# Self-attention denominators added up on Pool, and the context's split in the added tile's memory

## The chip, the cores and the metric

The kernel runs on one core of a Trainium2 chip. The metric is the device time of one execution in microseconds. A core has five engines with instruction queues of their own: TensorE (PE in the profile; PEld are its weight loads), VectorE (DVE), ScalarE (ACT), GpSimd (POOL, called Pool here) and SyncE (SP), which issues most of the transfers. An engine executes its instructions in the order in which they were written to its queue, and an instruction waits for semaphores of other engines and of transfers.

## The reference

Six stages work on x of shape (4, 512, 512) and a context of shape (4, 512, 128). Each adds its result to x and applies a layer norm:

```python
x = _layernorm(x + _L0_attn_ref(x, ...))            # causal self-attention, 16 heads of 32
x = _layernorm(x + _L0_xattn_ref(x, ctx, ctx))      # cross-attention, 32 query heads, 8 key heads of 16
x = _layernorm(x + _L0_ffn_ref(x, ...))             # feed-forward with ternary weights
x = _layernorm(x + _L1_attn_ref(x, ...))            # causal self-attention, 16 heads of 32
x = _layernorm(x + _L1_xattn_ref(ctx, x, ...))      # adjacency: similarity, top 153 of 512 in each row
x = _layernorm(x + _L1_ffn_ref(x, ...))             # 16 experts, two per token, and one shared
```

The change is in the two self-attentions and in the cross-attention. A causal self-attention computes, for every head, `softmax(q k / sqrt(32))` over the keys that are not later than the query, times v. The softmax is the exponential of each score less the row's maximum, divided by the sum of these exponentials over the keys (the denominator).

The adjacency stage takes its similarities from the context alone, so its selection of the largest 30% in each row (a bisection on a threshold) can be made at any time; the kernel makes it beside the self-attentions.

## The kernel before

**Self-attention.** Queries are on the free axis and keys on the partitions when the exponentials are taken, so the denominator is a sum over partitions, and that is a matmul with ones. The work is cut into 16 groups n for each layer: batch b = n // 4, and four heads, g = n % 4. The 512 keys are four tiles kb of 128. Since the attention is causal, tile kb meets only the queries from 128 kb on: the score tiles of four heads are 512, 384, 256 and 128 queries wide. A loop runs over steps t, four for each group. In each step the following is issued:

- `maxima` (line 230 and on): the scores of one tile of queries, with the queries on the partitions, for a row maximum. DVE reads them with the mask (L246) into `st`.
- at the group's first step, `least`: the negative maxima are turned on TensorE and copied by ScalarE (`nmT`, L269).
- `softmax(n, kb)`: five steps after the maxima, with kb in the order 2, 1, 0, 3. TensorE computes the scores with keys on the partitions, adds the negative maximum and the mask by matmuls, and ScalarE writes the exponentials (L296) into the tile `p` of this kb, two heads at a time.
- at the group's second step, `values(n - 2)`: first the denominators (matmuls of `ones` and `p` into a `tp` tile of PSUM, copied by ScalarE to `us`, L311), then, after the step's softmax, the products with the values (`va`) into `mm`. `finish` takes the reciprocals (L324) and multiplies (L325).
- projections of the next batch (q through DVE, L216; k through ScalarE, L220; v through DVE, L222) and the output projection of the last one, a part in every step. In the first steps it is those of batch 0.
- `background()`: one step of the selection.

The scores use three pairs of PSUM banks, and `mm` and `tp` one bank each, so a matmul into any of these waits until the engine that reads its bank has done so. The order of all matmuls on TensorE is fixed as they are issued (`in_order`; the profile shows all of them at the helper's line L424). The other engines' orders are made by a scheduler at build time, by its own costs.

**The background.** In the first self-attention `background()` begins with `split_context` (L436 and on). For each batch it loads the context into `ct` on SP's queue (L442), and Pool scales it (L443), writes a bf16 part (L446), subtracts it (L449), and so on, for three parts. Each part is sent to DRAM, `ctx_part` (L447). `ct` and the three parts `ct0` to `ct2` are four tiles of their own. Then the parts are arranged in DRAM as the cross-attention's keys: `keys[0]` by eight transfers (L452), and `keys[1]` by 20: four times 16 rows of the third part (L458), and 16 transfers of ones (L462) into the other rows, from a tile that Pool sets (L456). Then the selections of batches 0 and 1 follow; in the second self-attention it is those of batches 2 and 3, without a split. A selection computes similarities on TensorE (`sim`), takes the rows' largest and smallest on DVE, the first midpoint on Pool (`mid`, L1015 and L1016), and then, step by step, counts signs on ScalarE (L1023) and moves the midpoint on Pool (L1031 to L1035).

Pool also adds the output bias to x in the self-attentions (L193).

**Cross-attention.** At its start DVE sets the tiles `va0` and `va1` to ones (L490) and three small tiles `xl` to zeros (L494), beside the last layer norm of the self-attention (L339 to L349). For each batch the keys come back from DRAM as `ks` (from `keys[0]`, L498) and `kl` (from `keys[1]`, all 128 partitions, L499). Pool splits the queries (L527 to L531), TensorE multiplies, and DVE takes the maxima (L554).

The lines of the helper behind each kind of sums, in `values`:

```python
for to, left in ((t, None), (o, VA[b % 2])):
    for kb in range(NT):
        for j in range(NJ):
            multiply(to[HD * j : HD * (j + 1), kb * P :], ...)
```

Of the kernel before, what the change touches and what calls it, by code (L numbers as in the profile page):

```python
# [21 lines left out]
P = 128  # L22
# [18 lines left out]
def decoder_kernel(ctx: ExitStack, tc: tile.TileContext, a: dict, out: bass.AP):  # L41
# [39 lines left out]
    iota_i = const.tile([P, NE], mybir.dt.int32, tag="iotai", name="iota_i")  # L81
    G.iota(iota_i, pattern=[[1, NE]], base=0, channel_multiplier=0)
    iota = const.tile([P, NE], F32, tag="iota", name="iota")
    V.tensor_copy(iota, iota_i)
    thr = const.tile([P, B * NT], F32, tag="thr", name="thr")
    ctx_parts = [tc.dram_tile([P, B * S], BF16, name=f"ctx_part{k}") for k in range(3)]
    keys = [tc.dram_tile([P, 8, B * S], BF16, name=f"keys{k}") for k in range(2)]
# [48 lines left out]
    def self_attention(pre, first, background=lambda: None):  # L136
# [3 lines left out]
        with tc.tile_pool(name=pre + "w", bufs=1) as wp, tc.tile_pool(  # L140
# [130 lines left out]
            PR = {}  # L271
# [25 lines left out]

            def values(n):

                b, g = divmod(n, NG)  # L300
                o, t = psum_mm(), psum_tp().rearrange("p n t -> p (n t)")
                for to, left in ((t, None), (o, VA[b % 2])):
                    for kb in range(NT):
                        for j in range(NJ):
                            multiply(
                                to[HD * j : HD * (j + 1), kb * P :],
                                ones[:, :HD] if left is None else left[:, kb, NJ * g + j, :],
                                PR[n, kb][:, j, :], start=(kb == 0), stop=(kb == NT - 1),
                            )
                    u = po.tile([P, S], F32, tag="us" if left is None else "u", name="u", bufs=1)  # L310
                    A.copy(u, to)  # L311
                    if left is None:
                        sums = u
                        yield
                if g == 0:
                    O[b] = po.tile([P, NG, S], F32, tag="oT", name="oT", bufs=1)
                F[n] = sums, u
# [119 lines left out]
    def split_context(pool):  # L437


        for b in range(B):  # L440
            ct = pool.tile([P, S], F32, tag="ct", name="ct")
            nc.sync.dma_start(ct, a["ctxT"][:, ts(b, S)])  # L442
            G.tensor_scalar(ct, ct, 0.25, None, ALU.mult)  # L443
            for k in range(3):
                c = pool.tile([P, S], BF16, tag=f"ct{k}", name=f"ct{k}")
                G.tensor_copy(c, ct)  # L446
                nc.sync.dma_start(ctx_parts[k][:, ts(b, S)], c)  # L447
                if k < 2:
                    G.tensor_tensor(ct, ct, c, ALU.subtract)  # L449
            yield  # L450
        for p, k in enumerate(KPART):
            nc.sync.dma_start(  # L452
                keys[0][ts(p, XD)], ctx_parts[k].rearrange("(g d) t -> d g t", d=XD)
            )
        one = pool.tile([P, S], BF16, tag="ct0", name="ct0")
        G.memset(one, 1.0)  # L456
        for r in range(P // 32):
            nc.sync.dma_start(  # L458
                keys[1][32 * r : 32 * r + XD], ctx_parts[2].rearrange("(g d) t -> d g t", d=XD)
            )  # L460
            for b in range(B):
                nc.sync.dma_start(  # L462
                    keys[1][32 * r + XD : 32 * (r + 1), :, ts(b, S)],
                    one[:XD].unsqueeze(1).to_broadcast([XD, XG, S]),
                )
        yield
# [7 lines left out]
    def cross_attention(background):  # L474
        HD, NG, NJ, NP = XD, XG, 4, XP
        multiply, transpose = in_order()
        with tc.tile_pool(name="ck", bufs=1) as kp, tc.tile_pool(
# [8 lines left out]
            for k in range(2):  # L486
                KS.append(kp.tile([P, NG, S], BF16, tag=f"ks{k}", name=f"ks{k}"))
                KL.append(kp.tile([P, NG, S], BF16, tag=f"kl{k}", name=f"kl{k}"))
# [8 lines left out]
            def load(b):  # L497
                nc.sync.dma_start(KS[b % 2], keys[0][:, :, ts(b, S)])  # L498
                nc.sync.dma_start(KL[b % 2], keys[1][:, :, ts(b, S)])  # L499
# [931 lines left out]
    with tc.tile_pool(name="sims", bufs=1) as mp:  # L1431
        selection, background = selecting((0, 1), mp, split_context(mp))
        with psum(3, 1, 1):
            self_attention("L0", True, background)
# [19 lines left out]
    with tc.tile_pool(name="sims2", bufs=1) as mp:  # L1454
        selection, background = selecting((2, 3), mp)
        with psum(3, 1, 1):
            self_attention("L1", False, background)
# [51 lines left out]
```

## Time and profile before

| what | value |
|---|---|
| median of 3 runs | 2528.08 us (2526.78 to 2528.53) |
| profiled execution | 2531.25 us, its span 2529.5 us |
| mean granted TensorE clock | 0.958 |
| first self-attention | 0 to about 546 us of the span |
| cross-attention | from about 546 us |
| second self-attention | about 1420 to 1960 us |
| Pool, busy over the span | 629.6 us (25%) |
| all transfers | 163.74 MB |

The profile is that of one execution. Its page gives each engine's busy time, then groups of instructions by line, engine and tile, with the number of instructions, the mean time of one in nanoseconds, and the idle time ahead of them with what ended it. A timeline row gives the start, the length, the engine, the line, the operation with its tiles and shapes, how many instructions it joins, and in brackets the idle time before it with its releaser. The view of waits adds up what an engine waited for: microseconds in total, how often, and the longest. TensorE shows a float32 matmul as two records, so the 16 matmuls of one block of sums are 32 records.

### The profile page before, as it was taken

The page shows a single profiled execution, that of the slowest core. Times are in us where ns is not written, and L with a number is a line of the kernel's source. Part 1 is how long each engine was busy: PE and PEld are TensorE (multiplying, and loading weights), DVE is VectorE, ACT ScalarE, POOL GpSimd, SP SyncE. Part 2 cuts the span into 40 slices and gives each one's busy share as a digit, 9 for nine tenths or more (in the row PEclk, how much of TensorE's full clock was granted, in tenths as well). Part 3 has the DMA queues.
Part 4 walks back from the last instruction along what each step waited for, and adds up shares of the span by engine and source line. Part 5 has one row for each costly group of instructions (what it writes and reads, how often), then busy time and mean ns, then how long its engine had stood idle before and what let it go on. Part 6 is the DMA issues. An engine that isn't in the chain of part 4 may idle for free. (4 is left out here: it accounts for less than half of the span.)

```text
span 2529.5 us, 34778 instructions
## 1 busy us (share of the span) xinstructions
PE 2263.4 (89%) x13014; PEld 1006.0 (40%) x13014; DVE 1424.4 (56%) x3136; ACT 1105.4 (44%) x1744; POOL 629.6 (25%) x1218
## 2 busy tenths in 40 slices
PE   7899999878989899989998689989998898999996
PEld 2334333333333333345555234433444443444442
DVE  2455565547887878758887345546555741111117
ACT  0732643325767677665665273274323210122221
POOL 7300210033333333137766240031000031000005
PEclk9999999889999999999999799999998899999997
DMA  6500000037130401000000200000001241444536
GB/s 221 152 22 18 1 17 1 1 125 242 48 119 22 146 1 51 1 1 1 1 1 1 85 5 14 1 1 20 1 1 51 68 167 66 134 133 152 181 119 197
DMA packets 93436, 163.74 MB, mean 65 GB/s; under 512 B 7376, under 2 KB 39504, under 8 KB 93264
## 3 DMA queue, kind: packets, MB, share of 16 engines
q1 hardware_dynamic: 76000, 122.94, 14.8%
q10 hardware_dynamic: 12144, 21.77, 2.3%
q0 software_dynamic: 5120, 16.78, 2.0%
q8 instruction: 103, 1.69, 0.3%
q14 instruction: 69, 0.57, 0.1%
HBM read 163.30 MB, written 51.64 MB: 85 GB/s over the span
## 5 line engine op out<-in xcount | busy, mean ns | idle before, releaser
L554 DVE TENSOR_REDUCE nm<-sc 128x2 f32<-128x1024 f32 x256 | 304.2, 1218 | 99.1 <-PE sc L424 98.8
L592 ACT ACTIVATE p<-sc 128x1024 f32<-128x1024 f32 x256 | 248.4, 1023 | 138.9 <-PE sc L424 138.9
L246 DVE CUSTOM_DVE_ANT_0 e<-sc,late_keys 128x256 bf16<-128x256 f32 (+3 forms) x512 | 222.5, 484 | 128.3 <-PE sc L424 128.3
L296 ACT ACTIVATE p<-sc 128x512 f32<-128x512 f32 (+3 forms) x256 | 165.8, 700 | 213.3 <-PE sc L424 213.3
L424 PE MATMUL mm<-p,va 128*32 128x512 f32 (+3 forms) x2048 | 217.6, 528 | 0.7 <-ACT p L592 0.5
L1363 PE MATMUL sc<-wug,xbT 128*128 128x512 f32 x376 | 185.2, 600 | 17.3 <-ACT sl L1368 14.1
L424 PE MATMUL sc<-qs,ks 128*128 128x512 bf16 x512 | 151.7, 382 | 33.7 <-DVE nm L554 31.8
L424 PE MATMUL sc<-ks,qs 128*128 128x512 bf16 x512 | 157.2, 391 | 4.4 <-DVE nm L554 3.3
L424 PE MATMUL sc<-kT,qT 32*128 32x512 f32 (+3 forms) x1024 | 133.7, 498 | 24.5 <-ACT p L296 20.4
L424 PE MATMUL sc<-qT,kT 32*128 32x256 f32 (+3 forms) x1024 | 133.9, 509 | 17.4 <-DVE st L246 15.6
L324 DVE RECIPROCAL u<-u 128x128 f32<-128x128 f32 x128 | 108.4, 909 | 62.0 <-ACT u L311 62.0
L1360 DVE COPY xbT<-tp 128x512 f32<-128x512 f32 x47 | 32.2, 689 | 196.2 <-PE tp L1358 196.2
L1023 ACT ACTIVATE junk<-sim,mid 128x512 bf16<-128x512 f32 x176 | 124.9, 722 | 17.2 <-POOL mid L1016 17.2
L1397 POOL DMA_INDIRECT yg<-ys,pi x32 | 35.2, 1099 | 375.8 <-issue 373.4
L746 POOL TENSOR_TENSOR y<-z 128x512 f32<-128x512 f32 (+1 forms) x48 | 97.3, 2040 | 87.3 <-DVE z L731 87.2
L424 PEld LDWEIGHTS sc<-kT,qT 32*128 32x128 f32 x1024 | 51.8, 189 | 116.5 <-issue 73.4
L424 PEld LDWEIGHTS <-ks 128*128 128x128 bf16 x512 | 50.0, 98 | 117.2 <-issue 76.7
L746 POOL TENSOR_TENSOR z<-y 128x512 f32<-128x512 f32 x64 | 95.3, 1508 | 3.4 <-issue 2.1
L1363 PEld LDWEIGHTS sc<-wug,xbT 128*128 128x128 f32 x376 | 64.9, 190 | 77.5 <-issue 54.6
L424 PEld LDWEIGHTS sc<-qT,kT 32*128 32x128 f32 x1024 | 52.0, 193 | 97.7 <-issue 58.6
L1377 PE MATMUL sc<-wd,hT 128*128 128x512 f32 x188 | 88.3, 592 | 0.0
L743 ACT ACTIVATE g<-sc,sg 128x512 f32<-128x512 f32 x64 | 43.7, 685 | 94.0 <-PE sc L734 62.3
(297 smaller groups left out, 4175.8 us busy)
## 6 DMA issues: line engine op xcount, KB each, us to landing
wug<-in_Wu SPq DMA_DIRECT2D x47, 512.0 KB
wug<-in_Wg SPq DMA_DIRECT2D x47, 512.0 KB
wd<-in_Wd SPq DMA_DIRECT2D x47, 512.0 KB
xs<-zero SPq DMA_DIRECT2D x3, 4096.0 KB
xb<-xs SPq DMA_DIRECT2D x47, 256.0 KB
ys<-yb ACTq DMA_DIRECT2D x47, 256.0 KB
w<-in_w_gate SPq DMA_DIRECT2D x16, 512.0 KB
w<-in_w_up SPq DMA_DIRECT2D x16, 512.0 KB
```

Of the source, the lines that this page charges most:

```text
L246: V.tensor_tensor_reduce(e, at[r], late_keys[:, (NT - m) * P :], 1.0, LOWEST, ALU.add, ALU.max, accum_out=st[:, i, r : r + 1],)
L296: A.activation(heads, sc[h][:, :, :m], AF.Exp)
L324: V.reciprocal(sums[:, ts(i, P)], sums[:, ts(i, P)])
L424: ins = op(*args, **kw)
L554: V.tensor_reduce(NM[n][:, i, 2 * h : 2 * h + 2], sc, AX.X, ALU.max, negate=True)
L592: A.activation(p[:, 2 * h : 2 * h + 2, :], sc[h], AF.Exp)
L743: then(act, A.activation(*args, **kw))
L746: then(pool, getattr(G, op)(*args))
L1023: A.activation(e, s[k], AF.Sign, bias=bias[:, k : k + 1], accum_out=to[:, k : k + 1])
L1363: T.matmul(pp[:, 0, :], xbT[:, c, :], wug[s][:, c, :, :].rearrange("p q f -> p (q f)"), start=(c == 0), stop=(c == NK - 1),)
L1377: T.matmul(pp[:, 1, :], hT[:, c, :], wd[s][:, c, :], start=(c == 0), stop=(c == F // P - 1),)
L1397: G.indirect_dma_start(out=y, out_offset=None, in_=ys, in_offset=bass.IndirectOffsetOnAxis(pos[k][:, t : t + 1], 0),)
```

## The change

The change has three parts.

First, the denominators. For queries of 128 and on, Pool now adds up the exponentials of the key tiles 0, 1 and 2 in a new tile `R` of 128 x 4 heads x 384 queries (tag `r`, one buffer, in the pool that also holds the similarities). After the exponentials of kb = 1 it adds those of kb = 2 to them (two adds of 2 heads x 256 queries); after those of kb = 0 it adds these (for each pair of heads one add of 2x128, one of 2x256). So six adds for each group. `values` then multiplies ones by p of kb = 0 for the first 128 queries, by R for the 384 others, and by p of kb = 3 for the last 128: 640 columns instead of 1280 for each head, 12 matmuls instead of 16. The products with the values stay as they were.

Second, `ct` and its three bf16 parts are slices of one tile that has R's tag and so R's one buffer. All the split's tiles and all R share this memory, one after another. The small integer tile `iota_i` also moves to a pool that is closed at once.

Third, `keys[1]` keeps only the 16 rows of the third part in DRAM, written by one transfer. DVE sets both `kl` tiles to ones at the start of the cross-attention, and for each batch four transfers of 16 rows replace the one of 128.

```diff
-    iota_i = const.tile([P, NE], mybir.dt.int32, tag="iotai", name="iota_i")
...
+    with tc.tile_pool(name="int", bufs=1) as ip:
+        iota_i = ip.tile([P, NE], mybir.dt.int32, tag="iotai", name="iota_i")
...
-    keys = [tc.dram_tile([P, 8, B * S], BF16, name=f"keys{k}") for k in range(2)]
+    keys = [tc.dram_tile([n, 8, B * S], BF16, name=f"keys{n}") for n in (P, 16)]
...
                     A.activation(heads, sc[h][:, :, :m], AF.Exp)
 
+                for h in range(NJ // 2):
+                    heads = slice(2 * h, 2 * h + 2)
+                    if kb == 1:
+                        if not h:
+                            R[n] = tiles.tile([P, NJ, S - P], F32, tag="r", name="r")
+                        G.tensor_tensor(
+                            R[n][:, heads, P:], p[:, heads, P:], PR[n, 2][:, heads, :], ALU.add
+                        )
+                    elif kb == 0:
+                        r = R[n][:, heads, :]
+                        G.tensor_tensor(
+                            r[:, :, :P], PR[n, 1][:, heads, :P], p[:, heads, P : 2 * P], ALU.add
+                        )
+                        G.tensor_tensor(r[:, :, P:], r[:, :, P:], p[:, heads, 2 * P :], ALU.add)
...
-                    for kb in range(NT):
+                    if left is None:
+                        parts = [(PR[n, 0][:, :, :P], 0), (R.pop(n), 1), (PR[n, 3], 3)]
+                    else:
+                        parts = [(PR[n, kb], kb) for kb in range(NT)]
+                    for p, q in parts:
                         for j in range(NJ):
                             multiply(
-                                to[HD * j : HD * (j + 1), kb * P :],
-                                ones[:, :HD] if left is None else left[:, kb, NJ * g + j, :],
-                                PR[n, kb][:, j, :], start=(kb == 0), stop=(kb == NT - 1),
+                                to[HD * j : HD * (j + 1), q * P : q * P + p.shape[2]],
+                                ones[:, :HD] if left is None else left[:, q, NJ * g + j, :],
+                                p[:, j, :],
+                                start=q < (2 if left is None else 1),
+                                stop=q == NT - 1 or (left is None and q == 0),
                             )
...
         for b in range(B):
-            ct = pool.tile([P, S], F32, tag="ct", name="ct")
+            all_ = pool.tile([P, 4, S - P], F32, tag="r", name="ct").rearrange("p j t -> p (j t)")
+            ct = all_[:, :S]
...
-                c = pool.tile([P, S], BF16, tag=f"ct{k}", name=f"ct{k}")
+                c = all_[:, S + k * (S // 2) : S + (k + 1) * (S // 2)].bitcast(BF16)
...
-        one = pool.tile([P, S], BF16, tag="ct0", name="ct0")
-        G.memset(one, 1.0)
-        for r in range(P // 32):
-            nc.sync.dma_start(
-                keys[1][32 * r : 32 * r + XD], ctx_parts[2].rearrange("(g d) t -> d g t", d=XD)
-            )
-            for b in range(B):
-                nc.sync.dma_start(
-                    keys[1][32 * r + XD : 32 * (r + 1), :, ts(b, S)],
-                    one[:XD].unsqueeze(1).to_broadcast([XD, XG, S]),
-                )
+        nc.sync.dma_start(keys[1], ctx_parts[2].rearrange("(g d) t -> d g t", d=XD))
...
-                KL.append(kp.tile([P, NG, S], BF16, tag=f"kl{k}", name=f"kl{k}"))
+                t = kp.tile([P, NG, S], BF16, tag=f"kl{k}", name=f"kl{k}")
+                V.memset(t, 1.0)
+                KL.append(t)
...
-                nc.sync.dma_start(KL[b % 2], keys[1][:, :, ts(b, S)])
+
+                for r in range(NJ):
+                    nc.sync.dma_start(
+                        KL[b % 2][32 * r : 32 * r + HD], keys[1][:, :, ts(b, S)]
+                    )
```

## The prediction

> **What bounds the kernel now.** I read the page first, then TensorE's waits in the self-attentions, then the timeline at the places that the edits touch. Of the page, the busy shares, and three groups:
>
> ```profile
> PE 2263.4 (89%) x13014; PEld 1006.0 (40%) x13014; DVE 1424.4 (56%) x3136; ACT 1105.4 (44%) x1744; POOL 629.6 (25%) x1218
> ...
> L296 ACT ACTIVATE p<-sc 128x512 f32<-128x512 f32 (+3 forms) x256 | 165.8, 700 | 213.3 <-PE sc L424 213.3
> ...
> L193 POOL TENSOR_TENSOR x<-x,L0bo 128x512 f32<-128x512 f32 x16 | 19.7, 1264 | 0.0
> ```
>
> TensorE is busy 89% of the span. The exponentials (L296) wait only for it; the adds that Pool already makes (L193) give the price of the new ones: 1.26 us for 512 elements. Between 200 and 250 us of the first self-attention Pool does nothing, and TensorE never stops; the windows view (columns: window, PE, PEld, DVE, ACT, POOL, clock, DMA share, GB/s) says so, and shows a slow stretch early:
>
> ```profile
> 200.00:250.00 50.00, 50.00 (x288) 21.02 (x288) 24.75 (x82) 15.00 (x21) 0.00 (x0) 1.00 0.00 1
> ...
> 80.00:90.00 10.00, 9.12 (x37) 3.62 (x34) 1.55 (x8) 9.97 (x26) 4.91 (x27) 0.53 0.96 258
> ```
>
> So time taken from TensorE in the loop is time taken from the span, unless another engine is next. TensorE's waits from 100 to 520 us show who is next: ScalarE's exponentials and DVE's maxima, each only eight times:
>
> ```profile
> PE sc L424 <- ACT p L296: 8.9, 8, 2.4
> PE sc L424 <- DVE st L246: 8.6, 8, 1.5
> ```
>
> The sums block is the run of 32 records `tp<-p,ones`; the timeline at 226 us gives its length, 226.06 to 228.35, where the next scores begin:
>
> ```profile
> 226.06 2.36 PE L424 MATMUL tp<-p,ones 128*32 128x512 f32 x32
> 228.35 0.71 PE L424 MATMUL sc<-qT,kT 32*128 32x256 f32 x8
> ```
>
> The start of the stage is another matter. There Pool splits the context (L443 to L449) and then makes the first midpoint (L1015), ScalarE counts signs with it (L1023), then writes kT (L220), and TensorE waits for that kT:
>
> ```profile
> 63.22 0.61 POOL L446 CAST ct<-ct 128x512 bf16<-128x512 f32 x1
> 64.26 0.19 POOL L1015 TENSOR_TENSOR mid<-hi,lo 128x2 f32<-128x2 f32 x1
> 64.83 0.72 ACT L1023 ACTIVATE junk<-sim,mid 128x512 bf16<-128x512 f32 x1 [3.28 <-POOL mid L1016]
> 66.25 0.66 ACT L220 ACTIVATE kT<-mm,L0bk 128x512 f32<-128x512 f32 x1
> 66.97 3.27 PE L424 MATMUL mm<-xt,L0wq 128*128 128x512 f32 x7 [0.97 <-ACT kT L220]
> ```
>
> Today the chain costs TensorE 0.97 us. Whatever makes Pool's last split later, moves that matmul by as much.
>
> **The change, part by part.** The profiled execution took 2531.25 us (span 2529.5), 3.2 above the median of the runs, 2528.08; I sum against it and take 3.2 off at the end.
>
> *1. The sums.* A block passes widths 512, 384, 256 and 128 four times, each as two records. In the block at 226 us the weight loads mark the passes: 0.454 + 0.429 us for 512, 0.323 twice for 384, 0.216 twice for 256, 0.109 and a tail for 128: 2.29 us. Afterwards 128, 384, 128: 0.22 + 0.65 + 0.22 + 0.12 tail = 1.21. That is 1.08 us for each of 32 blocks: 34.4 us at most. What is late next: the scores behind the block wait for PSUM pairs that DVE frees with the four maxima (L246) of the step before. In a regular block the second maximum ends 1.15 us before the block does, so all is kept (about 16 of them). In six that run beside output projections (226, 363, 468, 1639, 1782, 1887 us) it ends 0.62 before (227.66 + 0.08 against 228.35, at 226), so half is kept. Around 109, 287, 321, 1677 and 1712 us ScalarE is counting signs, and TensorE stops for exponentials or copies behind the block (0.33 to 2.4 us); there I keep 0.3 each, at 1712 none. Together with the tail below: 10.1 us in the first self-attention, 10.9 in the second: **+21**. Bounds: 0 (Pool always late) and 34.
>
> *2. Pool's adds.* Four adds of 2x256 at 1.26 us and two of 2x128 at 0.67 (L529, 128x256) a block: 6.4 us, 205 in all, on an engine idle there. The last exponential of key tile 0 ends 6.40 us before the block that needs R (5.04 in one case); behind it Pool has 1.9 to 2.9 us of adds, so R is about 3.5 us early. Not at the tail of each layer, where no scores lie between: in the last block but one the exponentials end 0.53 us before, in the last after it. There R is late, 1.25 us lost and nothing gained (within the 10.1 and 10.9). DVE's own L246, L324 and L222 show no change beside Pool's L193; only L325 (0.69 to 1.76) and the small parts do, and they don't fall on the adds: 0, at worst -4 (1 us in some blocks).
>
> *3. Selection beside the adds.* The bisection's Pool steps (L1031 to L1035) queue behind adds. Six blocks are touched; a burst of 2.5 to 3.9 us of adds holds the next midpoint, so signs start 0.6 to 1.1 us late, and what follows them on ScalarE (exponentials) too: **-4**, between 0 (the signs have room) and -8 (TensorE takes all).
>
> *4. Splitting in R's memory.* Before, ct and its three parts are tiles of their own: the load of batch b+1 waits only for Pool's last read. Now all four are slices of one buffer, so that load (on SP's queue) waits until the three parts of batch b have landed; then the load, then Pool. The built order also puts the first midpoint behind all of Pool's splits. Batch 0 lands at about 23 to 24 us (19.63 before: it stands behind more loads on SP's queue), its last cast is near 36.5, and with the adds of x2 and x3 (L193, between) that of batch 1 near 54.5. Then for each batch: Pool 6.0 (57.84 to 63.83), landing of the last part about 1.9, load 3.3 (53.38 to 56.5 today; 5.1 when contended, 41.80 to 46.99): 11.2. The last cast comes at 77 instead of 63.8, the first sign at 77.7 instead of 64.83, and TensorE resumes 2.14 us later (64.83 to 66.97), at 79.9: **-12.9**, between -8 (landing and load at half) and -19 (both contended). Waits before it (2.16 us for scT at 31.41, 0.8 at 20 and 24) lie inside the stall and give nothing. After an idle stretch TensorE is slow: its first 8 matmuls at 13.27 took 5.89 us, the same 8 at 20.00 took 3.70; after 2.16 us idle two took 2.04, against 1.02: **-1.7** (0 to -2.2). Against that: the slow stretch at 80 to 90 us, where four matmuls of mm<-xt,L0wq took 3.78 us at 84.08 and 1.94 at 89.83, so about 4 us are lost; it follows TensorE's wait of 1.68 us for a maximum at 79.03. If the pause lets DVE catch up and the dip goes, +4; if it only moves, 0. I take 0, since the work around it comes in the same order.
>
> *5. The keys' ones.* SP loses 20 issues and 4 MB of transfers between 64 and 94 us: TensorE has no DMA wait there, so 0. In the cross-attention four loads of 0.13 MB replace one of 1 MB, a batch: 0, as no TensorE wait there ends with a load; -1 if the three more issues on SP (0.6 us each, as 546.43 to 547.09) delay cv, +1 if the spared bytes speed its neighbours. DVE gets two memsets, 128x4096 bf16, ahead of the last normalization. The nearest row:
>
> ```profile
> 547.25 0.91 DVE L490 MEMSET va<- 128x1024 f32 x1 [0.16 <-issue]
> ...
> 557.90 2.51 DVE L554 TENSOR_REDUCE nm<-sc 128x2 f32<-128x1024 f32 x2 [4.39 <-PE sc L424]
> ```
>
> 0.91 us for 1024 elements, or for 4096 bytes. By elements each memset takes 3.6 us, 7.3 together, and DVE, free from 553.5 for 4.39 us, starts L554 at about 560.8, 2.9 late; TensorE is paced by DVE from there: **-2.7**. By bytes, 1.8 each, 3.6 together, the idle time hides it. I take elements: DVE's L246 writes 512 bf16 in 0.69 us, and L339 writes 512 f32 in the same 0.69. Pool's copy into xl waits for its memset, 4 us later, but the block it feeds is needed past 570.
> The Trainium skill, "VectorE: DVE Perf Modes" (Zero memsets can be issued as uint32), says that a memset takes one cycle per element whatever the dtype, which speaks against this edit. By it the sum has -2.7 here; if bytes counted, 0. No row of before shows a memset to bf16 on DVE.
>
> **Sum.** 21 - 4 - 12.9 - 1.7 - 2.7 = -0.3 us. 2531.25 + 0.3 - 3.2 = 2528: no change, since two effects cancel.
>
> **The rivals.**
> *Faster: the startup's price is smaller.* Pool is not on TensorE's path from 100 us on, so the +21 stand; the stall falls to 8, and the dip at 80 us disappears: -0.3 + 4.9 + 4 = 8.6, **2520**; with bursts free too, 2516. For it: half of the per-batch 5.2 us is transfer, which the leaner queue may shorten. Against: the ct load took 5.1 us when it met other loads.
> *Slower: the startup chain.* One mechanism: part landing and reload, two batches in a row, each contended (3 and 5.1 instead of 1.9 and 3.3) put the last cast at 83, the stall at 19: 6 us more, **2534**; with batch 1 counted so too, 2537. It decides when the last cast ends later than 82 us.
> *Slower: Pool is late in every block,* the wait for R taking the place of the removed matmuls. It needs adds over twice as slow (3.5 us of slack against 1.9 to 2.9 of work); Pool's slowest plain add of this size is 1.81. Then +21 go: **2549**.
> **How the numbers follow.** 0.2% is 5 us, about what a measurement can tell from no change. Cancelling as summed: 0.45, its own range 2520 to 2535. Cheap startup: 0.28. Contended chain: 0.21. Late R: 0.06. Of the first, two thirds lie within 5 us; with edges of the others, same 0.37. Faster: 0.28 less what stays inside plus the first's edge, 0.30. Slower 0.33. The range leaves out the lowest of the second case and late R: 2513 to 2542.
>
> **What would show it.** Blocks `tp<-r,ones` of about 1.2 us, no TensorE waits for Pool's r but at the tails; a TensorE gap of 11 to 15 us before `mm<-xt,L0wq` at 67, ended by kT; the last ct cast near 77; a kl memset of 3.6 us and L554's first start near 561. Wrong if the block keeps 2 us, if Pool ends the waits in regular blocks, or if the gap near 67 is under 8 or over 19.

## The result and the profile after

| | median, us | lowest to highest | runs |
|---|---|---|---|
| before | 2527.97 | 2526.78 to 2528.53 | 4 |
| after | 2542.21 | 2537.48 to 2547.12 | 4 |

The ratio after / before is 1.0056, with a 95% interval of 1.0044 to 1.0069: the kernel became 14.2 us slower. The forecast was 2528, between 2513 and 2542, so the result lies just outside its range.

The profiled execution of the changed kernel took 2537.48 us, 4.7 below its median; that of before took 2531.25, 3.3 above its own. The two traces therefore show only a difference of 6.3 us. What the other 8 us are is taken up by the first experiment.

The page of the changed kernel, its engines and the group of Pool's new adds (columns of a group: line, engine, operation, shapes, count | busy us, mean ns of one | idle us ahead of them and what ended it):

```profile
PE 2243.2 (88%) x12758; PEld 999.5 (39%) x12758; DVE 1440.5 (57%) x3138; ACT 1106.1 (44%) x1744; POOL 831.2 (33%) x1409
...
L304 POOL TENSOR_TENSOR r<-p,p 128x512 f32<-128x512 f32 x64 | 80.2, 1276 | 368.9 <-ACT p L297 368.9
```

TensorE has 20 us less work, and Pool 202 more, an add costing 1.28 us. So part one does what it says, and the span is longer all the same.

The timeline of TensorE in the changed kernel, around the block of sums that began at 226 us before, one of the six beside output projections (start, length, engine, line, operation, count):

```profile
239.89 0.43 PE L447 MATMUL tp<-p,ones 128*32 128x128 f32 x8
240.13 0.83 PE L447 MATMUL tp<-r,ones 128*32 128x384 f32 x8
240.77 0.40 PE L447 MATMUL tp<-p,ones 128*32 128x128 f32 x8
241.11 1.00 PE L447 MATMUL sc<-qT,kT 32*128 32x256 f32 x6
```

From 239.89 to 241.11 are 1.22 us, where the block of before took 2.29 (226.06 to 228.35). TensorE's waits over most of the first self-attention's loop (117 to 531 us), in the changed kernel (what waits, for whom: us in total, times, longest):

```profile
PE sc L447 <- DVE st L247: 8.6, 8, 1.6
PE sc L447 <- ACT p L297: 7.0, 7, 2.1
...
PE tp L447 <- POOL r L312: 0.4, 1, 0.4
```

The first row is as before, and the second is a little less (8.9 us, 8 times, before). In this stretch Pool's `r` ends one wait only, at its end. So Pool keeps up in the loop. In the tail itself (500 to 560 us) the view has 2.2 us in three waits for `r`, the longest 1.1; the tail of layer 1 has the same 2.2.

To see where the time went, the same matmul was looked up in both traces, and its start before subtracted from its start after. The stages, by the times of before:

| stretch of before, us | after - before at its end | change in the stretch | what the forecast had |
|---|---|---|---|
| 0 to 75 (startup) | +15.1 | +15.1 | +14.6 |
| 75 to 500 (loop, layer 0) | +7.0 | -8.1 | -11.4, and a share of +4 |
| 500 to 553 (tail, layer 0) | +9.3 | +2.3 | +1.25 |
| 553 to 575 (two memsets) | +11.3 | +2.0 | +2.7 |
| 575 to 700 | +10.0 | -1.2 | 0 |
| 700 to 875 (cross-attention) | +14.9 | +4.9 | 0 |
| 875 to 1428 | +12.5 | -2.4 | 0 |
| 1428 to 1925 (loop, layer 1) | +1.4 | -11.1 | -12.1, and a share of +4 |
| 1925 to 2000 (tail, layer 1) | +6.7 | +5.3 | +1.25 |
| 2000 to the end | +6.3 | -0.4 | 0 |

**The startup.** The timeline of Pool, of ScalarE and of TensorE of the changed kernel (in brackets the idle time ahead, and its releaser):

```profile
24.78 1.52 POOL L467 TENSOR_SCALAR ct<-ct 128x512 f32<-128x512 f32 x1 [19.46 <-DMA ct<-in_ctxT]
...
60.59 1.49 POOL L467 TENSOR_SCALAR ct<-ct 128x512 f32<-128x512 f32 x1 [4.84 <-DMA ct<-in_ctxT]
...
71.21 1.49 POOL L467 TENSOR_SCALAR ct<-ct 128x512 f32<-128x512 f32 x1 [4.62 <-DMA ct<-in_ctxT]
...
76.58 0.61 POOL L470 CAST ct<-ct 128x512 bf16<-128x512 f32 x1
77.15 0.20 POOL L1035 TENSOR_TENSOR mid<-hi,lo 128x2 f32<-128x2 f32 x1
77.72 0.72 ACT L1043 ACTIVATE junk<-sim,mid 128x512 bf16<-128x512 f32 x1 [18.22 <-POOL mid L1036]
79.14 0.67 ACT L221 ACTIVATE kT<-mm,L0bk 128x512 f32<-128x512 f32 x1
79.86 5.87 PE L447 MATMUL mm<-xt,L0wq 128*128 128x512 f32 x8 [15.91 <-ACT kT L221]
```

Batches 2 and 3 wait 4.84 and 4.62 us for their load into the shared buffer, the last cast is at 76.58, and TensorE resumes at 79.86. Its wait of 15.91 us includes a lead of 2 us that it had gained by then. The eight matmuls behind the wait take 5.87 us instead of 3.70.

### The profile page after: what moved, and what is told of

It is laid out like the page before. It is cut to its first block, busy times and chain, and to the rows that moved or that the text cites. A ratio compares the mean times of both kernels' runs of the same rounds, so it can differ in the third digit from the quotient of the medians.

```text
span 2535.8 us, 34474 instructions
## 1 busy us (share of the span) xinstructions
PE 2243.2 (88%) x12758; PEld 999.5 (39%) x12758; DVE 1440.5 (57%) x3138; ACT 1106.1 (44%) x1744; POOL 831.2 (33%) x1409
## 5 line engine op out<-in xcount | busy, mean ns | idle before, releaser
L304 POOL TENSOR_TENSOR r<-p,p 128x512 f32<-128x512 f32 x64 | 80.2, 1276 | 368.9 <-ACT p L297 368.9
L447 PE MATMUL mm<-xt,L0wq 128*128 128x512 f32 x128 | 70.3, 682 | 32.2 <-ACT kT L221 15.9
```

Of the source, the lines that this page charges most:

```text
L304: G.tensor_tensor(R[n][:, heads, P:], p[:, heads, P:], PR[n, 2][:, heads, :], ALU.add)
L447: ins = op(*args, **kw)
```

## The experiments

Beside each run the kernel before ran again on the same chip, and a ratio is against these runs. Where a text on record speaks of theories by letter, its own words say which they are.

**The changed kernel again.** How much of the 14 us is chance?

> The changed kernel again, for a second trace. Theory A (waits): the lengthening is a fixed sum of waits, so the time is 2540 to 2544 us and a second trace lines up with the first within 1 us in every stage. Theory B (clock): the waits decide only where TensorE may fall to half clock, and chance decides whether it does; then the time spreads again over some 10 us (2537 to 2547), and the two traces differ by several us at places where one ran at half clock and the other did not, by about half of each such stretch.

Measured: 2543.56 against 2526.67, 1.0060 (1.0046 to 1.0074); single runs from 2538.65 to 2544.02. Its trace is 6.1 us longer than the first one. Part of the difference arises where TensorE's granted clock is 0.50 in one of the two and not in the other, in stretches such as 300 to 375 and 400 to 575 us. Added up, the clock was at half for 241.7 us in the first trace of the changed kernel, for 248.7 in this one, and for 213.2 in that of before. The 7.0 us more at half clock are worth at most 3.5 us (an estimate: full speed would do that work in half of the time). The rest lies in other places, such as 0.85 us at 625 us where both traces are at 1.00, and is not explained. The mean granted clocks say the same of the runs without a trace: 0.947 to 0.954 in these five of the changed kernel, 0.960 to 0.963 in the 16 of before. So the changed kernel runs at half clock longer, and its time varies from run to run. The pair of profiled executions hides that: the one of before had 0.958, a lower clock than any of these 16.

The terms of the table above come back in this second trace: the startup costs 14.6 us, the two tails 2.8 and 5.2, the stretch from 700 to 875 us 5.2. The loops gave less, 5.8 and 10.2.

**The split's slices in two buffers in turn.** Is it the shared buffer that stalls TensorE?

```diff
-            all_ = pool.tile([P, 4, S - P], F32, tag="r", name="ct")...
+            home, tag = (pool, "r") if b % 2 == 0 else (second[0], "p1")
+            all_ = home.tile([P, 4, S - P], F32, tag=tag, name="ct", bufs=1)...
```

> The split's slices alternate between R's buffer and the buffer of the exponentials' tile p1 (128x4x384, not yet in use then), so no load waits for the parts of the batch before it; the rest is the change as it is. Theory A (startup chain): TensorE's stop ahead of mm<-xt,L0wq at 80 us goes, 13 us and some 2 us of slow restart, so 2526 to 2529. Rival C (the stop is due to Pool's order, or something else holds kT): the stop stays over 8 us and the time stays at 2535 to 2543.

Measured: 2531.29, 1.0015 (1.0006 to 1.0024), 12.3 below the changed kernel beside it, and a little above the 2526 to 2529 of theory A. Pool waits for one load of `ct` only, the first, and TensorE does not stop ahead of the matmul that stood at 79.86; it starts at 71.23. It is still 4.2 us later than before. Pool's last cast is early enough now (55.42), and its first midpoint waits 7.4 us for DVE instead; behind that, TensorE had waited 7.25 us for the load of `scT` at 35.89, which it had for 2.16 at 31.41 before. So another transfer on SP's queue comes late here, of which more below.

**The shared buffer alone,** put into the kernel before; the ones' tile takes the same buffer.

```diff
-            ct = pool.tile([P, S], F32, tag="ct", name="ct")
+            all_ = pool.tile([P, 5 * S // 2], F32, tag="r", name="ct")
+            ct = all_[:, :S]
...
-                c = pool.tile([P, S], BF16, tag=f"ct{k}", name=f"ct{k}")
+                c = all_[:, S + k * (S // 2) : S + (k + 1) * (S // 2)].bitcast(BF16)
```

> The kernel before with one edit: ct and its three parts are slices of one buffer; sums and keys' ones as before. Theory A: the last cast comes 9 to 14 us later than 63.8, TensorE stops as long, and 2 us of slow restart come on top: 2538 to 2544. Rival C (the reload alone is hidden, it is the adds of R that matter): 2528 to 2532.

Measured: 2537.19, 1.0037 (1.0023 to 1.0050). In its trace it is 9.15 us late at 75 us and still 9.6 at 900; only about 3 us of it are made up by 1925. So little behind a startup stall gives it back. About 2 us of the stall are this run's own making: Pool's setting of the ones' tile waits 1.94 us for a part to land, which the change has no need to do. In the second self-attention's tail it loses another 3.4 us, with 10.2 us at half clock, though it has no R and no adds. So half clock can fall on that tail without them.

**The keys' ones alone,** set by DVE and not sent, in the kernel before.

```diff
-        one = pool.tile([P, S], BF16, tag="ct0", name="ct0")
...
+        nc.sync.dma_start(keys[1], ctx_parts[2].rearrange("(g d) t -> d g t", d=XD))
...
+                V.memset(t, 1.0)
...
-                nc.sync.dma_start(KL[b % 2], keys[1][:, :, ts(b, S)])
+                for r in range(NJ):
+                    nc.sync.dma_start(
+                        KL[b % 2][32 * r : 32 * r + HD], keys[1][:, :, ts(b, S)]
+                    )
```

> The kernel before with one edit: the keys' ones are set by DVE and not sent; sums and split as before. Theory A: two memsets of 3.6 us make the first maximum of the cross-attention 2.5 to 3 us late, partly caught up, and the four loads for each batch cost nothing: 2528 to 2531. Rival D (the four narrow loads for each batch hold up TensorE): 1 to 1.5 us at each of batches 1 to 3 more, 2531 to 2535.

Measured: 2536.84, 1.0038 (1.0025 to 1.0050), above both of the ranges given: about 10 us for a part that I had priced at 2.7. The waits of DVE in the cross-attention say where, for the weights of the feed-forward that it reads meanwhile. Before:

```profile
DVE wpart L686 <- DMA w<-in_w_gate: 1.2, 1, 1.2
DVE w L700 <- DMA w<-in_w_up: 1.2, 1, 1.2
DVE wpart L686 <- DMA w<-in_w_up: 0.6, 1, 0.6
DVE wpart L686 <- DMA w<-in_w_down: 0.3, 1, 0.3
```

With the ones set and four narrow loads for each batch:

```profile
DVE wpart L682 <- DMA w<-in_w_up: 3.5, 3, 1.9
DVE w L696 <- DMA w<-in_w_up: 3.3, 1, 3.3
DVE wpart L682 <- DMA w<-in_w_down: 1.4, 3, 0.6
DVE wpart L682 <- DMA w<-in_w_gate: 1.1, 1, 1.1
```

3.3 us of waits have become 9.3; the changed kernel has 8.7. DVE stands still in its queue, the cross-attention's maxima stand behind, and TensorE waits for these. The queue of SP, the wait of DVE and that of TensorE behind it, before:

```profile
702.45 1.31 SPq L680 DMA_DIRECT2D w<-in_w_up  x2
703.85 1.00 SPq L499 DMA_DIRECT2D kl<-keys  x1
...
710.40 2.56 DVE L686 TENSOR_REDUCE wpart<-w 128x1 f32<-128x1024 f32 x2 [0.59 <-DMA w<-in_w_up]
...
714.14 0.59 PE L424 MATMUL sc<-qs,ks 128*128 128x512 bf16 x2 [1.66 <-DVE nm L554]
```

And in this run:

```profile
701.08 1.27 SPq L676 DMA_DIRECT2D w<-in_w_up  x2
702.45 1.97 SPq L493 DMA_DIRECT2D kl<-keys  x2
...
710.33 1.22 DVE L682 TENSOR_REDUCE wpart<-w 128x1 f32<-128x1024 f32 x1 [1.92 <-DMA w<-in_w_up]
...
714.41 0.59 PE L424 MATMUL sc<-qs,ks 128*128 128x512 bf16 x2 [3.33 <-DVE nm L550]
```

Both loads of weights are issued ahead of the loads of `kl` in both kernels, and yet the first is read 9.2 us behind its issue, where it was 7.9. TensorE's wait is 1.7 us longer; the same happens at 846 us, where its wait goes from 2.21 to 4.31. Beside that the built order of DVE's and SP's instructions moved a little as well, and how much of the loss that makes is not separated.

The stretch from 700 to 875 us tells the loads apart in every trace. With narrow loads on SP's queue it costs 4.9 to 8.3 us (six traces, 5.8 in this one). With the wide load it costs between -0.1 and +1.0 in eight traces, and 3.0 in the first of the kernels with the sums alone, below. Not all of this run's time is of the loads: its trace also loses 4.4 us between 1200 and 1428, where nothing was edited.

**The two memsets alone,** in the kernel before.

```diff
-                KL.append(kp.tile([P, NG, S], BF16, tag=f"kl{k}", name=f"kl{k}"))
+                t = kp.tile([P, NG, S], BF16, tag=f"kl{k}", name=f"kl{k}")
+                V.memset(t, 1.0)
+                KL.append(t)
```

> The kernel before with DVE's two memsets of kl added, and the keys' ones sent and loaded as before (the loads overwrite all of it). Theory E (the narrow loads are the dearer half, through DVE's waits for the ternary weights): the memsets cost 3 us at the first maximum and 1.5 of it is caught up, so 2528 to 2530. Rival (the memset explains the whole loss of the keys' part): 2534 to 2538.

Measured: 2529.21 against 2527.59, 1.0007 (0.9998 to 1.0016). The trace loses 3.0 us between 553 and 575 us, and is 0.3 late behind 625. So the memsets cost 1 to 2 us, and the loads the larger part of the 10.

**The narrow loads on ScalarE's queue.** Is it that SP has 12 more issues ahead of the weights, or is it the transfers themselves?

```diff
                 for r in range(NJ):
-                    nc.sync.dma_start(
+                    nc.scalar.dma_start(
                         KL[b % 2][32 * r : 32 * r + HD], keys[1][:, :, ts(b, S)]
```

> The kernel before with the keys' ones set by DVE and not sent, as in the run with that edit alone, but the four narrow loads of kl for each batch go through ScalarE's queue instead of SP's, so that no load of the ternary weights stands behind them. Theory G (the place on SP's queue is the price): DVE's waits for the weights fall from 9.3 us to about the 3.3 of the kernel before, and only the memsets' 1 to 3 us are left: 1.0005 to 1.0015 of the kernel before. Rival H (the narrow transfers themselves slow the weights' transfers): DVE's waits stay at 7 us or more, and the ratio at 1.0025 to 1.0045.

Measured: 2549.41 against 2528.53, 1.0088 (1.0074 to 1.0103): worse than on SP's queue. DVE's waits:

```profile
DVE wpart L682 <- DMA w<-in_w_gate: 7.2, 4, 4.4
DVE wpart L682 <- DMA w<-in_w_up: 7.0, 3, 6.4
DVE w L696 <- DMA w<-in_w_up: 4.2, 1, 4.2
```

18.4 us now, with SP's queue free of these issues. The theory of the issues falls; what is left is the narrow loads in flight, beside which the weights' loads take longer. Part of the loss is of this run's own making, since ScalarE waits 7.7 us for another transfer (`xs<-zero`) near 574 us; but the stretch from 700 to 875 us alone costs 13.7. What in a transfer of 16 partitions makes its neighbours slow stays open.

**Part two undone within the change:** `ct` keeps R's buffer, the three parts take the buffers of `p3`, `p0` and `p1`.

```diff
-                c = all_[:, S + k * (S // 2) : S + (k + 1) * (S // 2)].bitcast(BF16)
+                c = homed(k, f"ct{k}")     # a tile of po with the tag "p3", "p0" or "p1"
```

> The change with its second part undone without new memory: ct lies in R's buffer, and the three parts in those of the exponentials' tiles p3, p0 and p1, each with its own wait as before the change. Theory A: no stop of TensorE at 67 to 80 us, and less of the 4 us that the two alternating buffers still lost ahead of 60 us: 2527 to 2531. Rival (the adds of R, not the split, lengthen the first stage): 2536 or more.

Measured: 2539.18 against 2527.59, 1.0037 (1.0025 to 1.0049). A miss: the startup still cost 9.9 us. The first split began at 24.59, against 19.63 before, so there was a cause ahead of any sharing. SP's queue showed it. The changed kernel has there, behind its first loads,

```profile
5.38 3.04 SPq L966 DMA_DIRECT2D swq<-in_L_xattn_Wq  x1
12.30 0.34 SPq L966 DMA_DIRECT2D swk<-in_L_xattn_Wk  x1
17.64 0.33 SPq L466 DMA_DIRECT2D ct<-in_ctxT  x1
```

and before

```profile
1.73 0.43 SPq L946 DMA_DIRECT2D swq<-in_L_xattn_Wq  x1
2.21 0.43 SPq L946 DMA_DIRECT2D swk<-in_L_xattn_Wk  x1
...
3.27 1.38 SPq L96 DMA_DIRECT2D x<-in_x  x1
8.87 0.34 SPq L442 DMA_DIRECT2D ct<-in_ctxT  x1
```

The load of `ct` is issued 8.8 us later. It stands behind two loads of weights for a later stage in both kernels; but before, these were issued at once, and in the changed kernel they wait: the first for DVE's copy of `iota_i` (0.8 us), the second till 12.30. The only edit of the change in that neighbourhood is the pool of `iota_i`, which is closed at once.

**`iota_i` in the memory of `thr`,** all else as in the changed kernel.

```diff
-    with tc.tile_pool(name="int", bufs=1) as ip:
-        iota_i = ip.tile([P, NE], mybir.dt.int32, tag="iotai", name="iota_i")
-        G.iota(iota_i, pattern=[[1, NE]], base=0, channel_multiplier=0)
-        V.tensor_copy(iota, iota_i)
     thr = const.tile([P, B * NT], F32, tag="thr", name="thr")
+    iota_i = thr.bitcast(mybir.dt.int32)
+    G.iota(iota_i, pattern=[[1, NE]], base=0, channel_multiplier=0)
+    V.tensor_copy(iota, iota_i)
```

> The change as it is, but the small integer tile iota_i lies in the memory of thr (the same size, used later) instead of in a pool that is closed at once, so that the load of swq waits for nothing and SP's queue begins in the old order. Theory F (a third of the startup's loss is SP's order): the first split starts near 19.5 instead of 24.8 us, the last cast comes at 69 to 72 instead of 77, and the time falls by 4 to 8 us, to 2535 to 2539. Rival (the reloads alone set the last cast): no change, 2541 to 2544.

Measured: 2537.55 against 2527.79, 1.0042 (1.0030 to 1.0055), where the changed kernel has 1.0056 and 1.0060; these intervals overlap, so the trace decides. The theory holds: SP issues the two loads of weights at 1.73 and 2.21 us again and `ct` at 8.88, and the timelines show

```profile
20.00 1.52 POOL L466 TENSOR_SCALAR ct<-ct 128x512 f32<-128x512 f32 x1 [14.66 <-DMA ct<-in_ctxT]
...
63.45 1.49 POOL L466 TENSOR_SCALAR ct<-ct 128x512 f32<-128x512 f32 x1 [5.31 <-DMA ct<-in_ctxT]
...
69.40 0.20 POOL L1034 TENSOR_TENSOR mid<-hi,lo 128x2 f32<-128x2 f32 x1
...
72.12 6.32 PE L446 MATMUL mm<-xt,L0wq 128*128 128x512 f32 x8 [7.68 <-ACT kT L220]
```

TensorE is 7.8 us late at 75, where the changed kernel is 15.1. About half of the startup's price is the late issue of `ct`, the other half the shared buffer's wait.

**The sums alone.** Three kernels keep part one and leave out parts two and three. The ones' tile needs a home in each, as the fourth buffer is gone, and the home matters.

The first put it into `p3`'s memory, with `iota_i` as in the change.

```diff
-        nc.sync.dma_start(keys[1], ctx_parts[2].rearrange("(g d) t -> d g t", d=XD))
+        one = homed(0, "one")     # tag "p3"
+        G.memset(one, 1.0)
+        for r in range(P // 32):
...
```

> The sums on Pool alone: the split's tiles as in the run before this one, and the keys' ones sent as before the change. By the traces so far the two self-attentions then gain 4.3 and 3.3 us net (blocks 11 to 13 us each, less bursts and tails), so 2517 to 2521. Rival (the narrow loads and the memsets are not what the cross-attention loses): the same time as the run before this one.

Measured: 2536.97, 1.0034 (1.0021 to 1.0047). A miss that tells little: the startup was 9.9 late by SP's order, and 18 us went at 109 us, where ScalarE's exponentials into `p` now stood behind signs of the selection: my placement of the ones had moved them.

The second took `iota_i` as above, and the memory of `y` for the ones.

```diff
+        one = pool.tile([P, S], F32, tag="y", name="one")[:, : S // 2].bitcast(BF16)
+        G.tensor_scalar(one, c, 0.0, 1.0, ALU.mult, ALU.add)
```

> The sums on Pool alone, with both startup effects undone: iota_i in thr's memory, ct in R's buffer, the three parts in those of p3, p0 and p1, the ones (written by a multiply by 0 and an add of 1 from the last part, so that they come after it) in the memory of the selection's tile y, and sent as before the change. SP's and Pool's orders are then those of the kernel before up to 64 us. Theory A: no stop at 67 us; the layers gain 4 to 7 and 3 us net: 2517 to 2521. Rival (the adds cost as much as they save, by late signs and half clock): 2525 to 2530.

Measured: 2531.49 against 2527.79, 1.0014 (1.0002 to 1.0026). The startup was repaired (+1.0 at 75). But the similarities' transfers on SP (`mixed<-sim`) moved from 130 to 206 us, and TensorE lost 14 us at 207 to 213. My placement again, not the change.

The third gave the ones the memory of `oT`; SP's order is then that of before.

```diff
+        one = homes[0].tile([P, 4, S], F32, tag="oT", name="one", bufs=1)
```

> The sums on Pool alone once more: as the two runs before, but the ones lie in the memory of the attention's result oT instead of the selection's tile y, so that the writes of sim to DRAM keep their place on SP's queue (they had moved from 130 to 206 us, and TensorE lost 14 us there). Theory A: those 14 us come back: 2515 to 2520. Rival (the loss at 207 us has another cause, or the sums gain nothing): 2528 to 2533.

Measured: 2536.66 against 2538.22, 0.9993 (0.9978 to 1.0007). (The runs of before beside it were 10 us longer than elsewhere, and its own trace loses 8.4 us at 2504 us, in the last stage, to a wait for DVE that no edit touches; the ratio is what counts.) The two tails still lose, with 2.2 us of waits for `r` in each: at 1925 us it is 6.8 ahead, at 2000 only 1.6.

**The same three, with the last two groups of each layer on TensorE.** There the adds lie on the path, since no scores stand between the exponentials and the sums.

```diff
-                for h in range(NJ // 2):
+                for h in range(NJ // 2 if n < total - LAST else 0):     # LAST = 2
...
-                    if left is None:
+                    added = left is None and n in R
+                    if added:
```

> As the run before this one, but the last two groups of each layer keep their 16 matmuls of ones and Pool adds nothing there. Theory A (R is late at the tail, and the half clock follows from it): 3 us in the first layer and 5 to 8 in the second come back, 2508 to 2514. Rival (the tail is slow by the clock's chance alone): within 2 us of the run before this one.

> As the run before this one, but the last two groups of each layer keep their 16 matmuls of ones, and Pool adds nothing there. Theory A (R late at the tail, with half clock after it): 2 to 3 us less in the first layer and 7 us in the second, 2508 to 2513. Rival (chance of the clock): within 2 us of the run before this one.

> As the run before this one, without Pool's adds and with the 16 matmuls in the last two groups of each layer. Theory A: 7 to 10 us less than that run, 2506 to 2511, and below the kernel before by 0.6 to 0.8%. Rival: as in the run before this one within 3 us.

| home of the ones | adds in all groups | without the last two groups |
|---|---|---|
| `p3` | 2536.97, 1.0034 | 2534.24, 1.0025 (1.0014 to 1.0035) |
| `y` | 2531.49, 1.0014 | 2521.57, 0.9976 (0.9967 to 0.9986) |
| `oT` | 2536.66, 0.9993 | 2529.44, 0.9961 (0.9946 to 0.9976) |

Leaving the tails alone gains 2.7, 9.9 and 7.2 us. The last two are as the theory had the difference, the first is not; and the times that the texts above give were missed in all three. The traces are clearer. From 1925 to 2000 us the eight with adds at the tail lose 5.0 to 7.7 us each; of the other traces, the four without adds there and three without any adds lie between -0.6 and +1.4, and only the shared buffer alone loses 3.3. The tail of layer 1 in the changed kernel, in the timeline of TensorE, shows a part of it:

```profile
1932.00 1.50 PE L447 MATMUL tp<-r,ones 128*32 128x384 f32 x4
1933.90 0.85 PE L447 MATMUL tp<-r,ones 128*32 128x384 f32 x2 [0.40 <-POOL r L312]
...
1947.02 0.84 PE L447 MATMUL tp<-r,ones 128*32 128x384 f32 x4 [0.70 <-POOL r L312]
...
1948.92 0.52 PE L447 MATMUL tp<-r,ones 128*32 128x384 f32 x2 [1.06 <-POOL r L312]
```

The waits for Pool are 2.2 us, of the 5.3 lost there. The windows view has the rest (columns: window, busy us and count of PE, PEld, DVE, ACT, POOL, then clock, DMA share, GB/s):

```profile
1917.20:1924.00 6.80, 5.79 (x73) 2.74 (x70) 5.45 (x13) 2.26 (x4) 0.00 (x0) 1.00 0.00 0
1924.00:1937.70 13.70, 13.28 (x94) 6.26 (x93) 4.10 (x14) 5.30 (x9) 6.34 (x6) 0.50 0.01 1
```

For 13.7 us the granted clock is 0.50. In the trace of before the same work ran at 1.00:

```profile
1916.00:1923.50 7.50, 6.48 (x89) 3.04 (x82) 5.46 (x13) 2.25 (x4) 0.00 (x0) 1.00 0.00 0
1923.50:1932.90 9.40, 8.03 (x98) 4.27 (x96) 2.13 (x13) 5.08 (x8) 0.00 (x0) 1.00 0.01 2
```

**The better one once more,** on another chip: sums on Pool except at the tails, the split's parts and the ones in `p`'s and `oT`'s memory, `iota_i` in that of `thr`, keys' ones sent as before.

> The sums on Pool without the tail, every queue in the old order, once more on whatever chip comes: if the gain is the kernel's and not that chip's, the ratio lies again between 0.9945 and 0.9975; if it was the chip's, between 0.998 and 1.001.

Measured: 2516.71 against 2528.53, 0.9953 (0.9939 to 0.9968). It beats both kernels, 11.8 us below before. Its page and the timeline at the two places:

```profile
PE 2239.9 (89%) x12790; PEld 1001.5 (40%) x12790; DVE 1441.5 (57%) x3136; ACT 1105.8 (44%) x1744; POOL 805.8 (32%) x1386
...
66.98 3.70 PE L451 MATMUL mm<-xt,L0wq 128*128 128x512 f32 x8 [1.68 <-ACT kT L224]
...
1917.02 2.36 PE L451 MATMUL tp<-p,ones 128*32 128x512 f32 x32 [0.52 <-ACT nmT L273]
```

The first matmul behind the split stands at 66.98, where it stood at 66.97 before, and the last but one block of sums takes its old 2.36 us without a wait for Pool.

## Why the prediction was wrong

Against the trace of before the forecast was +0.3 us, and the pair of traces has +6.3. Of the 6 us between them the startup makes 0.5, the loops 0.3, the two tails 5.1, the memsets -0.7, the narrow loads 4.9, what is caught up behind these two -3.6, and the end -0.4. So two terms failed in the traces, the tails of step 2 and the loads of step 5. The other 8 us, up to the medians, go with a lower clock in all runs of the changed kernel; that the clock makes them is not shown, and no step priced it behind the startup.

- **Step 1, the sums, held block by block.** 1.22 us against 1.21 forecast; regular blocks gain 1.07 or 1.08, as worked out, and the six beside output projections 0.57 each in the matmuls that follow, the half that was forecast. The loops gave 8.1 and 11.1 us, against 11.4 and 12.1 before the bursts of step 3.
- **The tail, in step 2, is a term that was mis-sized.** I had 1.25 us lost in each layer, by Pool's lateness. The traces have 2.3 and 5.3. The waits for R are 2.2 us in each layer; that is nearly the whole loss in layer 0, and in layer 1 the remainder falls into the stretch at half clock. Leaving the tails out gained 7 to 10 us in the two kernels whose startup was in order, and 2.7 in the third. That the waits bring on the half clock is not shown: the shared buffer alone had 10.2 us of it there too, without any R.
- **Pool's adds, in step 2, held but for the tail.** 1.28 us each, no wait for R in any regular block, so the rival of a late Pool is out.
- **Step 3** cannot be told apart exactly. What is missing in the two loops, 4.3 us, is near the 4 forecast, but holds half clock as well.
- **Step 4 was right in size, with half of its cause.** The last cast came at 76.58 (77 forecast), TensorE resumed at 79.86 (79.9), and the slow restart took 2.2 (1.7). The step had the late load of batch 0 in it, as standing "behind more loads on SP's queue", but took that for a part of the shared buffer. It is the closed pool of `iota_i`: putting it elsewhere gave back 7.3 us, and the shared buffer is left with 7.8. That the sum came out at 79.9 is therefore partly luck.
- **Step 5 is where the forecast broke.** The memsets were right: 3.47 us each against 3.6, and +2.0 against 2.7 in that place. The first maximum starts at 570.88; less the 9.3 us that the kernel is late by then, 561.6, for 560.8 in the working. The Trainium skill, "VectorE: DVE Perf Modes" (Zero memsets can be issued as uint32), says one cycle per element whatever the dtype, and the row agrees: 4096 elements of bf16 in 3.47 us are 0.85 ns each, and 1024 of float32 had taken 0.91 us. The timeline of the changed kernel:

```profile
557.97 3.47 DVE L503 MEMSET kl<- 128x4096 bf16 x1 [0.80 <-issue]
...
570.88 4.55 DVE L574 TENSOR_REDUCE nm<-sc 128x2 f32<-128x1024 f32 x4
```

  But the four narrow loads were priced at 0, "as no TensorE wait there ends with a load". They cost 4.9 us in the changed kernel's trace, and in the medians at most about 8.5 (10.2 for the ones alone, less 1.6 for the memsets). A load need not end a wait of TensorE: it ended one of DVE, for weights of the next stage, and the maxima behind it in DVE's queue ended TensorE's. In the trace of before DVE's waits for these weights, 3.3 us, were there to be read, and I had looked at TensorE's only.
- **Priced at the startup only** was the clock: 28 us more at half clock than before, even in the quicker of the two traces. At most half of this, 14 us, is time lost (an estimate, as above), and it lies inside rows of the table, the startup's and the tails' too. Single runs of the changed kernel differ by 10 us, the longest with the lowest clock (0.949) and the shortest with the highest (0.953). Why the clock falls more often stays open.
- **The rivals.** The cheap startup failed: its stall was full, and the slow stretch that began at 80 us only moved (+15.1 at 75, +16.4 at 126). The contended chain did not decide either, as the last cast came well before 82. The late R came at the tails alone. No case had the loads, or a clock that is lower throughout, in it.

The single parts do not add up either: -1.6 for the sums in `oT`'s version, +10.5 for the shared buffer, +10.2 for the ones and about +4 for `iota_i` (1.0042 against 1.0056 and 1.0060) make 23, and 14.2 were measured. In the changed kernel's trace some of the cross-attention's loss is caught up, 1.2 and 2.4 us, about 2 us of the run with the shared buffer are its own, and the startup's two causes lie in one chain; beyond that the remainder is open.

## What to carry to other kernels

Follow a moved transfer to every engine that waits in the same queue, not to the bottleneck's waits alone: here the loads that were edited ended no wait of TensorE, and reached it through VectorE's wait for other loads. Memory that is shared to save a buffer is a wait between tenants, and even a small tile in a pool that is closed at once changed which loads a queue could issue at once: compare the queues' issue orders and waits of the two builds before pricing anything behind them. And work taken off the bottleneck gains in the loop, where other work covers the replacement, but not at the loop's end; there the old way was worth 2.7, 9.9 and 7.2 us in three pairs of kernels.

## What the runs showed of the hardware that was not expected

- **The clock falls in steps of 3.4 us, with no plain rule.** In the tail of layer 1 the changed kernel had 13.7 us at 0.50, four times 3.42, behind a stretch with TensorE busy 5.79 of 6.80 us (85%); before had 6.48 of 7.50 us busy (86%) there, and stayed at 1.00. The Trainium skill, "TensorE: Matmul & The Clock Gate" (Part 1), states that half rate follows at least one idle window of about 3.4 us. The step agrees with these traces; the cause does not as far as these traces go, since no wait of TensorE in that stretch exceeds 1.01 us.
- **Narrow loads slow their neighbours.** Four loads of 128 KB into 16 partitions each, instead of one of 1 MB into 128, raised DVE's waits for 512 KB loads from 3.3 to 9.3 us, and to 18.4 from another queue, while half of the bytes fell away. The first of two such loads, issued ahead of them, was read after 9.2 us instead of 7.9. Why is open.
- **Single executions differ by as much as the effect.** The changed kernel ran between 2537.48 and 2547.12 us, with a mean granted clock of 0.953 down to 0.949, and one pair of traces showed 6.3 us of a difference of 14.2.
